# Turning whole float32 words: where a rotated q or k block is split into high and low parts, and how it travels to the stacks

## The chip, the cores and the metric

The kernel runs on one core of one Trainium2 chip. A core has a matrix engine (PE, whose weight loads are shown as a row of their own, PEld), a vector engine (DVE), an activation engine (ACT), a general engine (POOL), a queue engine that only issues transfers (SP), and 16 DMA engines that carry every transfer. The metric is the device time in microseconds of one execution, lower is better. A profile is one execution; the times are medians over several.

## The reference

A transformer block on x of shape 4 x 1024 x 256: attention with 16 heads of width 16 and rotary embedding, then a mixture of 8 experts, with a layer norm and a residual around each. The change touches only the rotated q and k and their way to the score products:

```python
q = (x @ Wq.T + bq).reshape(B, T, H, D)          # H = 16 heads, D = 16
k = (x @ Wk.T + bk).reshape(B, T, H, D)
q = apply_rope(q)                                # x1*cos - x2*sin, x1*sin + x2*cos
k = apply_rope(k)
scores = jnp.einsum('bthd,bshd->bhts', q, k) / np.sqrt(D)
attn = jax.nn.softmax(scores, axis=-1)
out = jnp.einsum('bhts,bshd->bthd', attn, v).reshape(B, T, C)
# then out @ Wo.T + bo, norm, residual, the expert layer, norm, residual
```

## The kernel before

**Tiling.** The attention is cut into 4 batches b, 4 groups g of four heads, and two halves of 512 tokens each. One unit is one (b, g, query half), so there are 32; each unit is done in 8 steps, one per 128 keys, so there are 256 steps (`step`, L709). A step issues on PE the score products `sc` of its four heads (L730), a second small product that subtracts each query's maximum (L736), the products `av` with the values of the step before (L805), and on the average four products `pm` of a unit ahead (L645), whose maxima over keys DVE takes (L648). ACT takes the exponential (L740).

**The stacks.** The score products run in a [...] format (`F32R`), and full precision is had by splitting each float32 word into a high part and a low part and laying both into the contraction: a head's 16 dimensions become 64 rows, q as (high, high, low, low) and k as (high, low, low, high). Those tiles are called stacks. For each (b, g, half) there are two pairs of heads `pr`, and for each pair one stack of q and one of k, of 128 rows x 512 words.

**The way of one half to its stacks**, before the change:

1. `rotated` (L524): five POOL operations on 128 x 512 words (bias, two products with sine, product with cosine, sum) give the tile `rot`, tokens on the partitions. Columns are four heads of q, then four heads of k.
2. `split` (L555): POOL copies `rot` into the even words of the tile `split` in the rounded format (high), then subtracts to get the low words beside them.
3. `stack` (L565): for q and for k separately PE turns four 128 x 128 blocks of interleaved high and low words (L572) into one PSUM bank `ps`, and ACT copies the bank to `half0` or `half1` (L580). A row of it is one dimension of one head, high or low.
4. SP issues ten transfers from SBUF to SBUF that lay those rows into the stacks (L592): per pair of heads, three of 64 rows and two of 32.

The first group (b = 0, g = 0) is done in a start-up stage (`begin`, L1024) with other hands: the rotation on DVE, the high part on ACT and the low part on DVE (`halved`, L1087), and half of the transfers issued from POOL (`fast`). The other 15 groups go through the loop, that is 30 halves.

**What sets the order.** The order on SP, PE, DVE and ACT is written out by hand, by a planner that runs while the kernel is built. A piece of work is a generator: each `yield` names what the next piece costs ("P430 A550" is 430 ns of PE, then 550 ns of ACT; W is a delay), and `run_one` (L452) fits the first due piece that finds its engines free by the planner's own clocks; two PE pieces a step at most (`QUOTA`, L790). `plan_stacks` (L1136) gives each half two pieces, the rotation and the stack: the stack comes after its rotation, the rotation of a half comes after the stack of the same half of the previous group, and both have a due step ahead of the first `pm` that reads the stack. POOL's vector work keeps the program's order (`InOrder`, L132); its transfers are set by the framework's scheduler. SP issues in program order, and on it stand also the copies of weights and empty rows in device memory that the first half of the loop spreads over the steps (L721).

**Buffers.** `rot`, `split`, `half0` and `half1` have two buffers each; PSUM gives four banks to `sc`, `ps` and the other turnings and copies that ACT empties, three to `pm` and what DVE empties, and one to `av`.

Of the kernel before, what the change touches and what calls it, by code (L numbers as in the profile page):

```python
# [8 lines left out]
F32 = mybir.dt.float32  # L9
I32 = mybir.dt.int32  # L10
F32R = mybir.dt.float32r
AF = mybir.ActivationFunctionType
ALU = mybir.AluOpType
# [3 lines left out]
P = 128  # L17
B, T, C = 4, 1024, 256
NH, HD = 16, 16
NG = 4  # L20
# [3 lines left out]
TB = 512  # L24
NTB = TB // P
# [32 lines left out]
def sandwich(  # L58
# [4 lines left out]
    nc = tc.nc  # L63
# [8 lines left out]
    pssc = attn.enter_context(tc.tile_pool(name="pssc", bufs=4, space=PSUM))  # L72
# [5 lines left out]
    ep1 = early.enter_context(tc.tile_pool(name="ep1", bufs=1, side="right"))  # L78
    ep2 = early.enter_context(tc.tile_pool(name="ep2", bufs=2, side="right"))

    def bank(name, pool=ps1):
        return pool.tile([P, TB], F32, tag="bank", name=name)
# [58 lines left out]
    pool = InOrder(nc.gpsimd)  # L141
# [403 lines left out]
        e.tensor_tensor(flat, flat, sw.rearrange("p t h s d -> p (t h s d)"), ALU.add)  # L545
        return c

    splits = {}

    def high_and_low(b, g, half):  # L550
        sp_ = ep2.tile([P, NTB, 8, HD, 2], F32R, tag="split", name=f"split_{b}_{g}_{half}")
        splits[b, g, half] = sp_
        return [sp_[:, :, :, :, l] for l in range(2)]

    def split(b, g, half):  # L555


        yield "G5500"
        c = rotated(b, g, half, pool)
        yield "G2100"  # L560
        hi, lo = high_and_low(b, g, half)
        pool.tensor_copy(hi, c)
        pool.tensor_tensor(lo, c, hi, ALU.subtract)

    def stack(b, g, half, fast=False):  # L565

        halves = []
        for is_k in range(2):
            yield "P430 A550"
            ps = bank(f"ps_{b}_{g}_{is_k}_{half}", pssc).bitcast(F32R)  # L570
            for t in range(NTB):
                nc.tensor.transpose(  # L572
                    ps[:, t * P : (t + 1) * P],
                    splits[b, g, half][:, t, 4 * is_k : 4 * is_k + 4].rearrange(
                        "p h d n -> p (h d n)"
                    ),
                    ident_r,
                )
            m = ep1.tile([P, TB], F32R, tag=f"half{is_k}", name=f"half{is_k}_{b}_{g}_{half}", bufs=2)
            (nc.vector.tensor_copy if fast and is_k else nc.scalar.copy)(m, ps)  # L580
            halves.append(m)
        yield "W8000"
        both = stack_tiles(b, g, half)
        stacks[b, g, half] = both
        for pr in range(2):
            q, k_ = (m[64 * pr : 64 * pr + 64] for m in halves)
            to_q, to_k = both[pr]
            for to, of in (
                (to_k[0::2], k_), (to_q[0::2], q), (to_k[1::4], k_[1::2]), (to_q[1::2], q),
                (to_k[3::4], k_[0::2]),  # L590
            ):
                (nc.gpsimd if fast and pr else nc.sync).dma_start(  # L592
                    out=to.bitcast(F32), in_=of.bitcast(F32)
                )

    def stack_tiles(b, g, half):
        if (b, g) == groups[-1]:
# [426 lines left out]
    def begin():  # L1024

        diag2 = ep1.tile([P, 2, 2, P], F32, tag="B", name="diag2", bufs=2)
        for r in range(2):
            for i in range(2):  # L1030
                nc.vector.tensor_scalar(diag2[:, r, i], ident, bqk_sb[:, i, 0:1], None, ALU.mult)
        pps = [[bank(f"pp_{h}_{n}", pssc) for n in range(2)] for h in range(2)]
        for pp in pps[0] + pps[1]:
            nc.tensor.matmul(
                pp, ones, diag2.rearrange("p r i c -> p (r i c)"), start=True, stop=False
            )
        turned_rope()
        diag = small_constants()
        columns = w2x.rearrange("p (i k) c -> p k i c", k=KC)
        scales = []  # L1040
        for h in range(NQB):
            stats = stats_tile(f"a0_{h}")
            statistics(stats, x_first[h], range(NTB))
            scales.append(norm_scales(stats, NTB, f"a0_{h}", pool if h else nc.vector))

        def normed(h):
            for n in range(2):
                xn = ep2.tile([P, 2, C], F32, tag="rot", name=f"xn_0_{h}_{n}")
                pt = bank(f"pt_0_{h}_{n}").rearrange("p (k t) -> p k t", k=KC)
                for i in range(2):  # L1050
                    normalized(xn[:, i], x_first[h][:, 2 * n + i, :], scales[h], 2 * n + i)
                    for k in range(KC):
                        nc.tensor.transpose(
                            pt[:, k, i * P : (i + 1) * P], xn[:, i, k * P : (k + 1) * P], ident
                        )
                nT = ep2.tile([P, KC, 2 * P], F32, tag="nT", name=f"nT_0_{h}_{n}", bufs=4)
                (nc.scalar.copy if h else nc.vector.tensor_copy)(nT, pt)
                norm[0, h * 2 + n] = nT

        def products(h, n):  # L1060
            for i in range(2):
                for k in range(KC):
                    nc.tensor.matmul(
                        pps[h][n][:, i * 2 * P : (i + 1) * 2 * P],
                        norm[0, h * 2 + n][:, k, i * P : (i + 1) * P], columns[:, k, :, :P],
                        start=False, stop=(i, k) == (1, KC - 1),
                    )


        parts = [  # L1070
            x_first[h].rearrange("p t (h s d) -> p t h s d", h=8, s=2) for h in range(NQB)
        ]
        cs = {}

        def times(h, n):
            t0 = h * NTB + 2 * n
            nc.vector.tensor_tensor(
                parts[h][:, 2 * n : 2 * n + 2].rearrange("p t h s d -> p t h (s d)"),
                pps[h][n].rearrange("p (t h d) -> p t h d", t=2, d=2 * HD),
                turn[:, t0 : t0 + 2, None, :].to_broadcast([P, 2, 8, 2 * HD]), ALU.mult,  # L1080
            )

        def rotation(h):
            cs[h] = ep2.tile([P, NTB, 8, HD], F32, tag="rot", name=f"rot_0_0_{h}")
            nc.vector.tensor_tensor(cs[h], parts[h][:, :, :, 0], parts[h][:, :, :, 1], ALU.add)

        def halved(h):  # L1087
            hi, lo = high_and_low(0, 0, h)
            nc.scalar.copy(hi, cs[h])
            nc.vector.tensor_tensor(lo, cs[h], hi, ALU.subtract)  # L1090

        normed(0)
        for n in range(2):
            products(0, n)
            times(0, n)
        rotation(0)
        normed(1)
        halved(0)
        products(1, 0)
        times(1, 0)  # L1100
        for _ in stack(0, 0, 0, fast=True):
            pass
        compact()
        products(1, 1)
        times(1, 1)
        rotation(1)
        halved(1)
        for h in range(NQB):
            turned[h] = turned_tile(0, h)
            others.append(Work(project(0, h, range(NTB), 1), h - 2))  # L1110
        for _ in range(2):
            others[0].run()
        for _ in stack(0, 0, 1, fast=True):
            pass
        turned_bias(diag)
        others[0].finish()
        matrices_of_maxima()
        for v in v_aug:
            pool.memset(v, 0.0)
            pool.memset(v[:, :, HD : HD + 1], 1.0)  # L1120
        for g in range(NG):
            for j in range(4):
                p0 = g % 2 * 64 + j * HD
                nc.sync.dma_start(
                    out=wo_sb[p0 : p0 + HD, g // 2, :], in_=wo[g, 32 * j : 32 * j + HD, :]
                )
        n = R2 - FR - 1
        nc.sync.dma_start(
            out=wall[:, FR + 1 : R2, OR:].rearrange("e p w -> p e w"),
            in_=zero[:n, None, :C].to_broadcast([n, NE, C]),  # L1130
        )
# [4 lines left out]
    def plan_stacks():  # L1136
        for k, (b, g) in enumerate(groups):
# [4 lines left out]
            for h in range(NQB):  # L1142
                deps = []
                deps.append(stacking[(*groups[k - 1], h)])
                if h:
                    deps.append(splitting[b, g, 0])
                if k == 1:
                    deps.append(others[h])
                if g == 0 and b:
                    preparing[b, h] = Work(  # L1150
                        prepare(b, h), drawing[b, g] - 22 + 6 * h,
                        after=[splitting[(*groups[k - 1], h)]]
                        + ([preparing[b, 0]] if h else []),
                    )
                    deps.append(preparing[b, h])
                splitting[b, g, h] = Work(
                    split(b, g, h), drawing[b, g] - (16 if g == NG - 1 else 6), after=deps
                )
            for h in range(NQB):

# [457 lines left out]
```

## Time and profile before

| quantity | value |
|---|---|
| time, median of 3 runs | 1631.56 us (1630.38 to 1631.83) |
| the profiled execution's own time | 1639.77 us |
| its span, first to last instruction | 1638.0 us |
| instructions | 27716 |
| DVE, ACT, POOL busy, share of the span | 64%, 52%, 31% |
| mean share of the 16 DMA engines, all transfers on SP's queue | 42.1% |

How to read it. A row of groups gives the line, engine and operation, output and inputs by tile name, the shape and the number of instructions, then their busy time together and the mean of one, and last the idle time of the engine just before them with what ended it. Matmuls overlap each other on PE, so the busy time of a group is less than its count times its mean; what one piece of work really costs on a full PE is read from a timeline, as the distance from its start to the start of what follows. The span falls into a start-up until 60 us, the attention loop until about 1030 us, the expert tiles until about 1580 us and a tail.

Busy time by stage, from the view by windows (us of each engine):

| stage | PE | DVE | ACT | POOL | DMA share |
|---|---|---|---|---|---|
| 60 to 1030 | 933.90 | 755.64 | 689.17 | 368.85 | 0.41 |
| 1030 to 1580 | 548.58 | 218.32 | 132.05 | 100.28 | 0.59 |
| 1580 to 1638 | 1.14 | 41.67 | 16.16 | 0.96 | 0.56 |

### The profile page before, as it was taken

How to read it: one execution, taken by the hardware profiler on the slowest of the kernel's cores; microseconds unless marked ns; L12 is line 12 of the kernel's file. 1: busy time of each engine (PE TensorE's matmuls, PEld its weight loads, DVE VectorE, ACT ScalarE, POOL GpSimd, SP SyncE). 2: the span in 40 equal slices, each digit the busy share in tenths (PEclk: the TensorE clock that was granted, in tenths of full speed). 3: DMA queues.
4: the chain of work that ended last, by engine and by line, in shares of the span. 5: the costliest groups of instructions: out<-in, count | busy, mean ns of one | idle time of the engine just before them, and what ended most of it. 6: DMA issues, size and time to landing. Idle time of an engine off the chain costs nothing. (4 is left out here: it accounts for less than half of the span.)

```text
span 1638.0 us, 27716 instructions
## 1 busy us (share of the span) xinstructions
PE 1532.8 (94%) x9456; PEld 1004.4 (61%) x9456; DVE 1046.5 (64%) x2511; ACT 854.8 (52%) x1754; POOL 513.2 (31%) x951
## 2 busy tenths in 40 slices
PE   7889999999999999999999999999999999999960
PEld 4444455645545554445554444788888888899950
DVE  4686788787788787868788883434434433334348
ACT  3366777677777767767677667322311111222213
POOL 6652152254372344462243112133230111111100
PEclk9899999999999999999999999999999999999985
DMA  4299887246054232212141042145455555788855
GB/s 121 90 247 237 236 237 186 85 117 177 12 132 136 75 103 80 53 52 65 37 94 40 1 159 87 66 167 203 179 183 195 195 194 221 251 312 300 304 226 199
DMA packets 114036, 247.94 MB, mean 151 GB/s; under 512 B 16772, under 2 KB 76967, under 8 KB 108007
## 3 DMA queue, kind: packets, MB, share of 16 engines
q1 hardware_dynamic: 103287, 215.47, 42.1%
q0 software_dynamic: 9120, 26.38, 4.9%
q10 hardware_dynamic: 1488, 4.33, 0.7%
q8 instruction: 75, 1.23, 0.3%
q14 instruction: 66, 0.54, 0.1%
HBM read 149.18 MB, written 80.73 MB: 140 GB/s over the span
## 5 line engine op out<-in xcount | busy, mean ns | idle before, releaser
L648 DVE TENSOR_REDUCE part<-pm 128x1 f32<-128x512 f32 x1024 | 640.5, 683 | 134.1 <-PE pm L645 132.1
L740 ACT ACTIVATE e<-sc 128x512 f32<-128x512 f32 x1024 | 530.2, 604 | 149.0 <-PE sc L736 147.5
L1330 PE MATMUL pu<-xT,w 128*128 128x256 f32 (+3 forms) x2024 | 359.9, 333 | 2.4 <-DMA w<-wall 1.2
L1330 PEld LDWEIGHTS pu<-xT,w 128*128 128x128 f32 (+1 forms) x2024 | 313.7, 190 | 33.2 <-issue 1.6
L1336 ACT ACTIVATE sil<-pu,w 128x256 f32<-128x256 f32 (+3 forms) x276 | 117.1, 425 | 415.9 <-PE pu L1330 392.9
L645 PE MATMUL pm<-stack,stack 64*128 64x512 f32 x992 | 282.5, 465 | 15.0 <-DVE part L648 11.9
L805 PE MATMUL av<-e,v 128*32 128x512 f32 x2048 | 274.9, 606 | 0.3 <-ACT e L740 0.3
L1341 DVE SCALAR_TENSOR_TENSOR h<-pu,w,sil 128x256 f32<-128x256 f32 (+1 forms) x230 | 97.2, 423 | 221.5 <-ACT sil L1336 220.6
L645 PEld LDWEIGHTS pm<-stack,stack 64*128 64x128 f32 x992 | 136.5, 185 | 162.1 <-DVE part L648 111.1
L730 PE MATMUL sc<-stack,stack 64*128 64x512 f32 x992 | 220.1, 405 | 4.1 <-ACT half L580 3.6
L736 PE MATMUL sc<-shift,bring 64*128 64x512 f32 x1024 | 222.7, 398 | 0.5 <-ACT shift L632 0.2
L1377 POOL DMA_INDIRECT res<-yo,ids x71 | 68.8, 969 | 411.7 <-DVE yo L1376 406.3
L1364 PE MATMUL pe<-w,h 128*128 128x256 f32 x710 | 167.5, 383 | 0.0
L1364 PEld LDWEIGHTS pe<-w,h 128*128 128x128 f32 x710 | 132.6, 190 | 25.4 <-issue 8.3
L730 PEld LDWEIGHTS sc<-stack,stack 64*128 64x128 f32 x992 | 113.8, 186 | 37.9 <-ACT e L740 15.0
L736 PEld LDWEIGHTS sc<-shift,bring 64*128 64x128 f32 x1024 | 105.7, 185 | 21.4 <-ACT shift L632 5.2
L1376 DVE TENSOR_SCALAR yo<-pe,xt 128x256 f32<-128x256 f32 x71 | 34.4, 484 | 90.3 <-PE pe L1364 90.2
L805 PEld LDWEIGHTS av<-e,v 128*32 128x32 f32 x2048 | 40.8, 108 | 71.1 <-issue 65.5
L992 POOL DMA_INDIRECT rows<-xr,to x64 | 62.6, 978 | 55.9 <-DVE to L987 34.6
L139 POOL TENSOR_TENSOR t_y<-y_y 128x4 f32<-128x4 f32 x24 | 4.7, 197 | 182.2 <-DVE y_y L334 181.0
L503 PE MATMUL pp<-wqk,nT 128*128 128x512 f32 (+1 forms) x128 | 61.1, 604 | 0.0
L139 POOL TENSOR_TENSOR rot<-turned,bias_qk 128x512 f32<-128x512 f32 x30 | 39.2, 1307 | 67.0 <-ACT turned L508 66.9
(297 smaller groups left out, 1396.2 us busy)
## 6 DMA issues: line engine op xcount, KB each, us to landing
w<-wall SPq DMA_DIRECT2D x46, 2034.0 KB
rows<-empty SPq DMA_DIRECT2D x35, 1032.0 KB
stack<-half SPq DMA_DIRECT2D x186, 128.0 KB
stack<-half SPq DMA_DIRECT2D x124, 64.0 KB
xt<-rows SPq DMA_DIRECT2D x25, 258.0 KB
wall<-in_wg_dram SPq DMA_DIRECT2D x16, 342.0 KB
wall<-in_w_dram SPq DMA_DIRECT2D x16, 320.0 KB
wall<-in_w_dram SPq DMA_DIRECT2D x8, 640.0 KB
```

The lines of the kernel that those rows point to most:

```text
L645: nc.tensor.matmul(pm, q[r, i * P : (i + 1) * P], k_[r], start=True, stop=True)
L648: nc.vector.tensor_reduce(part[:, i, 2 * pr + s, half : half + 1], pm, AX.X, ALU.max)
L730: nc.tensor.matmul(sc, k_[r, kt : kt + P], q[r], start=True, stop=False)
L736: nc.tensor.matmul(scs[s], bring[pr][r, :], shift[u][r, :], start=False, stop=True)
L740: nc.scalar.activation(e, scs[s], AF.Exp, scale=1.0 / HD**0.5)
L805: nc.tensor.matmul(av[32 * j : 32 * j + 32, :], v_aug[kb][:, 4 * g + j, :], es[j], start=(kb == 0), stop=(kb == NT - 1),)
L992: sent = nc.gpsimd.indirect_dma_start(out=rows[:, :], out_offset=bass.IndirectOffsetOnAxis(ap=to[:, i, t : t + 1], axis=0), in_=xr[:, t, i ...
L1330: nc.tensor.matmul(pu[:m, i, :n], w[:, c0 : c0 + m], xT[:, k, :n], start=(k == 0), stop=(k == KC - 1),)
L1336: nc.scalar.activation(sil[:m, :n], pu[:m, 0, :n], AF.Silu, bias=w[:m, OB + f : OB + f + 1])
L1341: nc.vector.scalar_tensor_tensor(h[:, f, :n], pu[:, 1, :n], bias, sil[:, :n], ALU.add, ALU.mult)
L1364: nc.tensor.matmul(po[:, :C], hs[j % 2][:, f, i * P : (i + 1) * P], w[:, O2 + f * C : O2 + (f + 1) * C], start=False, stop=(f == NC - 1),)
L1377: sent = nc.gpsimd.indirect_dma_start(out=res[:, :], out_offset=bass.IndirectOffsetOnAxis(ap=ids, axis=0), in_=y, in_offset=None,)
```

## The change

The split moves behind the turning. The rotated tile is turned as float32 words, all eight blocks of heads at once: four turnings of 128 x 128 into one PSUM bank instead of eight into two. In the loop ACT copies the bank to a new tile `full`, and POOL then makes the high part `part0` and the low part `part1` from it. In the start-up ACT rounds the bank straight into `part0`, and DVE subtracts it from the bank into `part1`; `halved` goes away. A row of `part0` or `part1` is one dimension of one head, so a pair of heads has 32 rows of q and 32 of k in each, and every quarter of every stack is one transfer: 16 transfers of 32 rows for each half, k before q, where there were six of 64 rows and four of 32. The bytes that they carry are the same. The stack's second piece now asks the planner for POOL time.

```diff
-    def high_and_low(b, g, half):
-        sp_ = ep2.tile([P, NTB, 8, HD, 2], F32R, tag="split", name=f"split_{b}_{g}_{half}")
...
-    def split(b, g, half):
+    def rotate(b, g, half):
         yield "G5500"
-        c = rotated(b, g, half, pool)
-        yield "G2100"
-        hi, lo = high_and_low(b, g, half)
-        pool.tensor_copy(hi, c)
-        pool.tensor_tensor(lo, c, hi, ALU.subtract)
+        rots[b, g, half] = rotated(b, g, half, pool)

     def stack(b, g, half, fast=False):
-        halves = []
-        for is_k in range(2):
-            yield "P430 A550"
-            ps = bank(f"ps_{b}_{g}_{is_k}_{half}", pssc).bitcast(F32R)
-            for t in range(NTB):
-                nc.tensor.transpose(
-                    ps[:, t * P : (t + 1) * P],
-                    splits[b, g, half][:, t, 4 * is_k : 4 * is_k + 4].rearrange(
-                        "p h d n -> p (h d n)"
-                    ),
-                    ident_r,
-                )
-            m = ep1.tile([P, TB], F32R, tag=f"half{is_k}", name=f"half{is_k}_{b}_{g}_{half}", bufs=2)
-            (nc.vector.tensor_copy if fast and is_k else nc.scalar.copy)(m, ps)
-            halves.append(m)
-        yield "W8000"
+        yield "P540 A550"
+        ps = bank(f"ps_{b}_{g}_{half}", pssc)
+        for t in range(NTB):
+            nc.tensor.transpose(
+                ps[:, t * P : (t + 1) * P],
+                rots[b, g, half][:, t].rearrange("p h d -> p (h d)"), ident,
+            )
+        parts = [
+            ep2.tile([P, TB], F32R, tag=f"part{i}", name=f"part{i}_{b}_{g}_{half}") for i in range(2)
+        ]
+        if fast:
+            nc.scalar.copy(parts[0], ps)
+            nc.vector.tensor_tensor(parts[1], ps, parts[0], ALU.subtract)
+        else:
+            full = ep2.tile([P, TB], F32, tag="full", name=f"full_{b}_{g}_{half}")
+            nc.scalar.copy(full, ps)
+            yield "G2100 W9600"
+            pool.tensor_copy(parts[0], full)
+            pool.tensor_tensor(parts[1], full, parts[0], ALU.subtract)
         both = stack_tiles(b, g, half)
         stacks[b, g, half] = both
         for pr in range(2):
-            q, k_ = (m[64 * pr : 64 * pr + 64] for m in halves)
-            to_q, to_k = both[pr]
-            for to, of in (
-                (to_k[0::2], k_), (to_q[0::2], q), (to_k[1::4], k_[1::2]), (to_q[1::2], q),
-                (to_k[3::4], k_[0::2]),
-            ):
-                (nc.gpsimd if fast and pr else nc.sync).dma_start(
-                    out=to.bitcast(F32), in_=of.bitcast(F32)
-                )
+            for is_k in (1, 0):
+                r = slice(64 * is_k + 32 * pr, 64 * is_k + 32 * pr + 32)
+                for n, low in enumerate(((0, 0, 1, 1), (0, 1, 1, 0))[is_k]):
+                    (nc.gpsimd if fast and pr else nc.sync).dma_start(
+                        out=both[pr][is_k][n::4].bitcast(F32), in_=parts[low][r].bitcast(F32)
+                    )
...
         def rotation(h):
-            cs[h] = ep2.tile([P, NTB, 8, HD], F32, tag="rot", name=f"rot_0_0_{h}")
-            nc.vector.tensor_tensor(cs[h], parts[h][:, :, :, 0], parts[h][:, :, :, 1], ALU.add)
-
-        def halved(h):
-            hi, lo = high_and_low(0, 0, h)
-            nc.scalar.copy(hi, cs[h])
-            nc.vector.tensor_tensor(lo, cs[h], hi, ALU.subtract)
+            rots[0, 0, h] = ep2.tile([P, NTB, 8, HD], F32, tag="rot", name=f"rot_0_0_{h}")
+            nc.vector.tensor_tensor(rots[0, 0, h], parts[h][:, :, :, 0], parts[h][:, :, :, 1], ALU.add)
...
-        halved(0)
...
-        halved(1)
...
                 splitting[b, g, h] = Work(
-                    split(b, g, h), drawing[b, g] - (16 if g == NG - 1 else 6), after=deps
+                    rotate(b, g, h), drawing[b, g] - (16 if g == NG - 1 else 6), after=deps
                 )
```

More of the change, by code (lines that the diff above doesn't have):

```diff
@@ L546, in rotated @@
         return c
-    splits = {}
-    def high_and_low(b, g, half):
-        sp_ = ep2.tile([P, NTB, 8, HD, 2], F32R, tag="split", name=f"split_{b}_{g}_{half}")
-        splits[b, g, half] = sp_
-        return [sp_[:, :, :, :, l] for l in range(2)]
-    def split(b, g, half):
-        yield "G5500"
-        c = rotated(b, g, half, pool)
-        yield "G2100"
-        hi, lo = high_and_low(b, g, half)
-        pool.tensor_copy(hi, c)
-        pool.tensor_tensor(lo, c, hi, ALU.subtract)
-    def stack(b, g, half, fast=False):
-        halves = []
-        for is_k in range(2):
-            yield "P430 A550"
-            ps = bank(f"ps_{b}_{g}_{is_k}_{half}", pssc).bitcast(F32R)
-            for t in range(NTB):
-                nc.tensor.transpose(
-                    ps[:, t * P : (t + 1) * P],
-                    splits[b, g, half][:, t, 4 * is_k : 4 * is_k + 4].rearrange(
-                        "p h d n -> p (h d n)"
-                    ),
-                    ident_r,
-                )
-            m = ep1.tile([P, TB], F32R, tag=f"half{is_k}", name=f"half{is_k}_{b}_{g}_{half}", bufs=2)
-            (nc.vector.tensor_copy if fast and is_k else nc.scalar.copy)(m, ps)
-            halves.append(m)
-        yield "W8000"
+    rots = {}
+    def rotate(b, g, half):
+        yield "G5500"
+        rots[b, g, half] = rotated(b, g, half, pool)
+    def stack(b, g, half, fast=False):
+        yield "P540 A550"
[17 more added lines that the diff above has]
+            pool.tensor_tensor(parts[1], full, parts[0], ALU.subtract)
         both = stack_tiles(b, g, half)
@@ L1072, in begin @@
         ]
-        cs = {}
         def times(h, n):
```

## The prediction

> **What bounds the kernel.** I read the stages by windows first, the groups of PE next, then the timeline of a few steps of the loop. In the loop PE is busy 933.90 of 970 us, in the expert stage 548.58 of 550; DVE comes second with 755.64 of 970. Whether a full PE is really the limit is seen in a step:
>
> ```profile
> 502.64 0.53 PE L572 MATMUL ps<-ident_r,split 128*128 128x128 f32 x4
> 503.10 0.50 PE L645 MATMUL pm<-stack,stack 64*128 64x512 f32 x2
> 503.44 0.39 PE L730 MATMUL sc<-stack,stack 64*128 64x512 f32 x2
> ...
> 504.81 1.06 PE L805 MATMUL av<-e,v 128*32 128x512 f32 x8
> 505.81 0.53 PE L572 MATMUL ps<-ident_r,split 128*128 128x128 f32 x4
> 506.27 0.50 PE L645 MATMUL pm<-stack,stack 64*128 64x512 f32 x2
> ```
>
> No row carries a wait, each piece begins as the one before drains, and the step from 502.64 to 505.81 lasts 3.17 us. Without the turning L572 it would be 3.17 - 0.46 = 2.71, which is what the step from 508.97 to 511.68 shows. So a PE piece taken out of the loop shortens it, until DVE (four maxima of about 0.62 us, 2.48 a step) comes near. How seldom PE waits stands in the groups:
>
> ```profile
> L645 PE MATMUL pm<-stack,stack 64*128 64x512 f32 x992 | 282.5, 465 | 15.0 <-DVE part L648 11.9
> L730 PE MATMUL sc<-stack,stack 64*128 64x512 f32 x992 | 220.1, 405 | 4.1 <-ACT half L580 3.6
> L572 PE MATMUL ps<-ident_r,split 128*128 128x128 f32 x240 | 34.3, 267 | 4.2 <-POOL split L139 4.1
> ```
>
> The column behind the last bar is PE's idle time: 12 us for DVE in the whole run, 3.6 for a PSUM bank that ACT's copy of a turned half holds, 4.1 for POOL's split.
>
> **The change part by part.**
>
> *Turning (L572).* 240 turnings in the loop are 60 banks of four; a bank costs 0.46 us from its start to the `pm` behind it, so a half costs 0.92-0.93. The change has one bank per half, of unrounded float32. The trace has that form: L675 turns four 128 x 128 float32 blocks.
>
> ```profile
> 475.57 0.66 PE L675 MATMUL pd<-ident,ou 128*128 128x128 f32 x4
> 476.16 0.51 PE L645 MATMUL pm<-stack,stack 64*128 64x512 f32 x2
> ```
>
> That is 0.59; others of L675, L827 and L483 before a `pm` give 0.53 to 0.57 where nothing else waits. I take 0.56: 0.93 - 0.56 = 0.37 saved a half, times 30 = **-11.1 us**; ends 0.34 and 0.47, so -10 to -14.
>
> Here a rule speaks against the change. The Trainium skill (FP8 and Floating Point Precision, "TensorE Precision Notes") says that true float32 takes four passes through the array, where the reduced format takes one. By the rule a float32 bank would cost 4 x 0.46 = 1.84 us (an estimate from that page), a half would lose 0.9 us, and 30 halves +27 us. The row decides: 0.53 to 0.59, a factor near 1.2, not 4, for a turning.
>
> *ACT.* One copy of a bank (about 0.59 us) less per half. ACT has room (689 of 970), so the time itself is worth nothing; but the bank waits of 3.6 us (five in the loop: 1.56 at 97.61, the others 0.43 to 0.71) come from two `ps` banks per half among four. One bank instead of two: I take half, **-1.8** (ends 0 and -3.6).
>
> *POOL's split moves behind the turning.* Its cost stays (cast 0.65, subtraction 1.30, a little under 2 us). In front of PE it goes away:
>
> ```profile
> 459.13 0.54 PE L572 MATMUL ps<-ident_r,split 128*128 128x128 f32 x4 [1.72 <-POOL split L139]
> ...
> 723.54 0.53 PE L572 MATMUL ps<-ident_r,split 128*128 128x128 f32 x4 [2.35 <-POOL split L139]
> ```
>
> With the rotation alone to wait for, POOL is done 2 us earlier; but the planner puts the turning earlier as well. I take half of 4.1, **-2** (ends +2 and -4). The new wait is on POOL: its cast waits for ACT's copy, and behind it stand the next rotations, the small operations of the norms and the indirect writes of rows. Such a block is there already, because the split's two buffers are held by PE:
>
> ```profile
> POOL split L139 <- PE ps L572: 68.6, 4, 26.4
> POOL rot L139 <- ACT turned L508: 66.9, 7, 25.9
> ...
> SPq L592 <- ACT half L580: 274.7, 22, 48.3
> ```
>
> These are total, times, longest. The same turning ends POOL's wait before and after, so it is replaced and not added. With POOL at 369 of 970 us its queue catches up.
>
> *Transfers.* Ten issues become sixteen on SP, and what waits behind them is the bulk copying of L721. The shortest cover is that of the first group:
>
> ```profile
> 79.88 6.23 SPq L592 DMA_DIRECT2D stack<-half  x10
> 86.16 0.59 SPq L721 DMA_DIRECT2D rows<-empty  x1
> 87.39 8.39 SPq L592 DMA_DIRECT2D stack<-half  x10
> ```
>
> Ten issues take 6.2 us, 8.4 where bulk copies fill the DMA engines (0.91 of their time from 90 to 120). Sixteen at the same pace are 10.0 and 13.4. The first set ends near 89, the second near 104. Their first `pm` stand at 101.93 and 113.46; landing took 2.0 to 4.2 us where the trace shows it (POOL's issues), and a bulk copy of 1 MB in front adds some 4. Cover left: 5 us and 2 us at worst. From the second group on, 37 to 84 us lie between the last issue and the first `pm`. So the six added issues cost **0**; without that cover the second set would stall PE for what it is late, a few us, once.
>
> The skill's other rule here (DMA: Bandwidth & Descriptors, "Rules for kernel authors") is to coalesce small transfers, since each carries a fixed 2 us. Priced serially, 6 x 30 x 2 = 360 us (an estimate from that page); by the rows an added issue is 0.6 us of SP, which idles 275 us in L592 alone. The rows decide.
>
> *Start-up.* ACT and DVE each lose one operation of about 0.69 per half, PE turns 0.6 instead of 0.84 and need not wait for the split (0.32 and 0.49), so PE reaches its first `pm` about 1 us before 35.39. POOL then issues eight transfers per half instead of five, at 0.53 each with a 1.86 us memset between: the last of half 0 leaves near 33.3, lands near 36.6, and the third `pm` waits 1 to 2 us. Together **0** (ends -1.5 and +2).
>
> *What is late next.* DVE. Its share in the loop is 78%, so I give back a fifth of what PE saves on it, **+2.4**.
>
> Sum: -11.1 - 1.8 - 2 + 0 + 2.4 = **-12.5 us** against 1639.77, that is 1627.3, or 0.76%. The expert stage is full on PE and shifts as it is. The median before is 1631.56, so the forecast is **1619 us**.
>
> **The rivals.**
>
> *No change to speak of: DVE takes the saving.* In favour: in units with norms and routing DVE has its own work beside 2.48 us of maxima per step, and a `pm` waits for its bank. Against: only 12 us of PE idle time end in DVE. If DVE took four fifths of the saved time, 2.5 us would be left: 1629. Chance 0.10.
>
> *Slower: PE meets late rotations.* One mechanism, at the turning of L572. POOL runs in program order, and each rotation of a group now comes behind the split of the group before, which waits for PE and ACT; before, the five operations of the rotation ran ahead and only the split waited. A rotation then starts when the last turning is done, and PE, in order too, stands at the next until it is there. The price is that of the two rows above, about 2 us a time. It decides from about 7 of 30 halves on (14 us); at half of them it is 15 x 2 - 12.5 = some +17, 1649. Against: in about three of four halves 20 to 60 us lie between the end of the split and its turning (rows of POOL's tile `split` against rows of L572), so a later start has room. Chance 0.12.
>
> *Stacks late in the first group only.* By the second set above, if its last transfers land 5 us behind their `pm` at 113 us: 1619 + 5 = 1624. Chance 0.13; still faster.
>
> *It doesn't do what it says* hardly arises: the count of turnings is in the code.
>
> **How the numbers follow.** Forecast 0.65 (own range 1612 to 1625), late first stacks 0.13, no change 0.10, late rotations 0.12. The measurement tells 0.2%, 3.3 us, from nothing. Faster: 0.65 + 0.13 = 0.78; within: 0.10; slower: 0.12. The range holds the forecast, the late first stacks and the no-change case: 1610 to 1632. Its low end is the sum of the good ends: -14 - 3.6 - 4 - 1.5 + 2.4 = -20.7.
>
> **What would show it.** Right: 120 turnings of L572's successor in the loop at about 0.56 us per bank, a loop shorter by 10 to 15 us in the stage up to 1030, no PE wait before `pm` at the first group, POOL's busy time unchanged, SP's issues still near 0.6 us. Wrong: PE idle before the turning ended by POOL's `rot` in many halves, idle before `pm` or `sc` that grows by ten us or more (DVE), or a bank of float32 turnings near 0.9 us or above.

## The result, and the profile after

The change makes the kernel slower: 1684.22 us (median of 6 runs, 1680.22 to 1686.84) against 1631.69 (6 runs, 1630.38 to 1637.47), a ratio of 1.0315 [1.0302, 1.0328]. The profiled execution took 1686.84 us with a span of 1685.0; its PE clock averaged 0.959 of full speed, where before it was 0.976. The expert stage only shifts: from the last `av` to the last `pe` lie 552.9 us after and 555.3 before. The loss lies in the attention loop, whose span from the first to the last `av` went from 951.2 to 1004.9 us, +53.7. (The first `av` also came 4.0 us sooner, at 70.50 for 74.54; but in b_lin below, whose start-up is that of before, it stands at 70.95, so this is not put down to the change.) "In the loop" means between these two `av` from here on, with the gaps under 0.15 us that the view of waits leaves out.

The groups of the profile after that answer to those shown before:

```profile
L636 PE MATMUL pm<-stack,stack 64*128 64x512 f32 x992 | 284.0, 475 | 35.1 <-DVE part L639 30.2
L721 PE MATMUL sc<-stack,stack 64*128 64x512 f32 x992 | 218.4, 415 | 0.0
L561 PE MATMUL ps<-ident,rot 128*128 128x128 f32 x128 | 22.0, 300 | 18.6 <-POOL rot L139 18.6
L139 POOL CAST part<-full 128x512 fp32r<-128x512 f32 x30 | 18.4, 613 | 129.4 <-ACT full L573 86.6 <-DMA rows<-empty 34.5 <-DMA stack<-part 8.3
```

Half as many turnings; the wait of `sc` for ACT's copies is gone; but the idle time before `pm` went from 15.0 to 35.1 and that before the turning from 4.2 to 18.6. PE's own waits, first of the kernel before, then of the one after (total us, times, longest):

```profile
PE pm L645 <- DVE part L648: 12.8, 30, 1.1
PE pmx L628 <- DVE mx L624: 10.0, 8, 1.8
...
PE ps L572 <- POOL split L139: 4.1, 2, 2.4
PE sc L730 <- ACT half L580: 3.6, 5, 1.6
```

```profile
PE pm L636 <- DVE part L639: 30.6, 32, 4.6
PE ps L561 <- POOL rot L139: 18.6, 4, 8.1
PE pbias__3509 L258 <- DMA lined<-lin: 18.1, 1, 18.1
PE pmx L619 <- DVE mx L615: 10.1, 6, 1.8
```

Three rows carry the loss: a few waits for DVE's maxima (`part`) of up to 4.6 us where none was over 1.1; four for a rotation; and one of 18.1 us for a transfer that the prediction never named.

**The four late rotations.** The timeline of POOL and PE at the first of them:

```profile
71.50 0.66 PE L561 MATMUL ps<-ident,rot 128*128 128x128 f32 x4
...
72.84 0.61 POOL L139 CAST part<-full 128x512 fp32r<-128x512 f32 x1 [16.00 <-ACT full L573]
73.53 1.28 POOL L139 TENSOR_TENSOR part<-full,part 128x512 fp32r<-128x512 f32 x1
74.76 1.30 POOL L139 TENSOR_TENSOR rot<-turned,bias_qk 128x512 f32<-128x512 f32 x1
...
78.95 1.26 POOL L139 TENSOR_TENSOR rot<-rot,sw 128x512 f32<-128x512 f32 x1
...
80.26 1.12 PE L561 MATMUL ps<-ident,rot 128*128 128x128 f32 x4 [4.82 <-POOL rot L139]
```

POOL stood 16 us in front of the cast until PE had turned that half and ACT had copied it; only then came the five operations of the next rotation, and PE, in order, stood at its turning. The next turning, at 87.60, waits 2.68 us more while POOL, busy without a pause, works off the same backlog. These two are the mechanism of the slower rival. The other two late rotations, 2.95 and 8.11 us, are not:

```profile
204.07 1.31 POOL L139 TENSOR_TENSOR rot<-turned,bias_qk 128x512 f32<-128x512 f32 x1 [25.87 <-ACT turned L508]
...
209.60 1.05 PE L561 MATMUL ps<-ident,rot 128*128 128x128 f32 x4 [2.95 <-POOL rot L139]
```

```profile
852.50 0.85 POOL L139 DMA_DIRECT2D xb<-in_x_dram  x1
853.35 0.62 POOL L139 CAST part<-full 128x512 fp32r<-128x512 f32 x1
...
860.75 1.12 PE L561 MATMUL ps<-ident,rot 128*128 128x128 f32 x4 [8.11 <-POOL rot L139]
```

At 204.07 POOL had waited for the rotation's own input; the rotation takes 5.5 us from there, and PE is free for its turning at 206.65. At 853.35 no split waits; the rotation, begun at 855.28, stands behind residual sums, splits and a norm's small operations that POOL does one after another since 840.00.

**The transfer.** SP's queue before, then after (start, duration from the first to the last issue of a row, number of issues):

```profile
255.38 6.24 SPq L592 DMA_DIRECT2D stack<-half  x10
...
263.02 8.59 SPq L592 DMA_DIRECT2D stack<-half  x10
271.71 1.06 SPq L249 DMA_DIRECT2D lin<-flat  x2
275.72 0.30 SPq L253 DMA_DIRECT2D lined<-lin  x1
```

```profile
232.53 35.77 SPq L712 DMA_DIRECT2D rows<-empty  x12
268.42 27.45 SPq L583 DMA_DIRECT2D stack<-part  x32
...
297.29 2.35 SPq L249 DMA_DIRECT2D lin<-flat  x2
303.67 0.30 SPq L253 DMA_DIRECT2D lined<-lin  x1
```

`lined` is the experts' biases on their way to a turning of PE (L258). Before, its transfer was issued at 275.72 and PE turned it at 281.29 without a wait. After, two sets of stacks are 32 issues instead of 20, the queue is late by 28 us, and PE stands for 18.1.

**The clock.** The clock record of the trace shows half speed for 3.4 us of the loop before and 71.7 after, in stretches of 3.4 us or a multiple. They stand behind the waits (windows: start:end, length, PE, PEld, DVE, ACT and POOL busy, granted clock, DMA share, GB/s):

```profile
291.60:312.10 20.50, 6.49 (x30) 3.85 (x30) 2.15 (x4) 2.74 (x7) 0.00 (x0) 0.50 0.52 127
349.70:356.50 6.80, 4.94 (x21) 2.30 (x21) 5.92 (x15) 0.61 (x2) 6.56 (x8) 0.50 0.94 286
854.80:865.00 10.20, 4.25 (x20) 2.75 (x24) 1.53 (x3) 2.11 (x5) 7.49 (x8) 0.50 0.46 134
```

The first is the wait for `lined`, the second one for DVE, the third the longest one for a rotation.

So the 53.7 us come apart: PE idle in the loop 31.2 before and 80.4 after, +49.2; PE busy 920.0 and 924.5, +4.5. If the turnings took some 11 us off the busy time, as the prediction's sum has it, about 16 came back; against x2_again below, which runs the same instructions on PE and is busy 913.0 us, it is 11.5. The clock is enough for either: PE was busy in 48.5 of the 71.7 us at half speed (before, in all 3.4), and there two products of a step stand 0.43 us apart (355.17 and 355.60) where at full speed it is 0.24 (472.42 and 472.66). 45.1 x (1 - 0.24 / 0.43) is an estimate of 20 us if every piece stretched so.

### The profile page after: what moved, and what is told of

Read it like the earlier page. It is cut to its first block, busy times and chain, and to the rows that moved or that the text cites. A ratio compares the mean times of both kernels' runs of the same rounds, so it can differ in the third digit from the quotient of the medians.

```text
span 1685.0 us, 27669 instructions
## 1 busy us (share of the span) xinstructions
PE 1530.3 (91%) x9328; PEld 1001.5 (59%) x9328; DVE 1054.4 (63%) x2509; ACT 838.2 (50%) x1722; POOL 515.0 (31%) x957
## 5 line engine op out<-in xcount | busy, mean ns | idle before, releaser
L636 PE MATMUL pm<-stack,stack 64*128 64x512 f32 x992 | 284.0, 475 | 35.1 <-DVE part L639 30.2
L721 PE MATMUL sc<-stack,stack 64*128 64x512 f32 x992 | 218.4, 415 | 0.0
L721 PEld LDWEIGHTS sc<-stack,stack 64*128 64x128 f32 x992 | 112.3, 193 | 26.9 <-ACT e L731 11.8
L139 POOL CAST part<-full 128x512 fp32r<-128x512 f32 x30 | 18.4, 613 | 129.4 <-ACT full L573 86.6
```

Of the source, the lines that this page charges most:

```text
L636: nc.tensor.matmul(pm, q[r, i * P : (i + 1) * P], k_[r], start=True, stop=True)
L721: nc.tensor.matmul(sc, k_[r, kt : kt + P], q[r], start=True, stop=False)
```

## The experiments

Ratios are against the kernel before on the same chip. **A plan** here means the order and place that the planner gives to all pieces of the loop. In a_lin, b_16 and b_lin that order is, on PE, DVE and ACT, the one of the kernel that they are made from; in x1_plan it is that of before less the operations that went. The traces bear this out: without the turnings and their copies, DVE and ACT run the same operations in the same order, and PE differs by swaps of neighbouring products alone.

**The transfer alone, and another hand for the split** (both from the kernel after).

```diff
# a_lin
-            nc.sync.dma_start(            # lin, twice
+            nc.gpsimd.dma_start(
-        lined = cl.tile([2 * NE, FF], F32, tag="xr", name="lined")
-        nc.sync.dma_start(out=lined, ...)
+        lined = cl.tile([2 * NE, FF], F32, tag="lined", name="lined")
+        nc.gpsimd.dma_start(out=lined, ...)
```

> The changed kernel with the three transfers that turn the biases (lin, lin, lined; L249 and L253) issued from POOL instead of SP, and with a buffer of its own for lined, so that they no longer stand behind SP's bulk copies and stack transfers, nor wait for the last copy of empty rows. PE, DVE and ACT keep their order. Theory (SP's queue is late): the one wait of 18.1 us at 305 us goes, and with it most of the 20 us of half clock around it, worth some 8 us more: about 1658 us. Rival (the order of the planner costs the time, and the wait only stands where something else would wait): above 1675 us.

Measured 1669.6 us, 1.0219 [1.0198, 1.0240]. The wait for `lined` is gone, worth about 15 us (1.0315 less 1.0219), and the rest stays: PE waits 30.4 us for `part`, 14.6 for rotations, half clock is 71.7 us. The time lies between the theory and the rival: more than two thirds of the loss have another cause.

```diff
# a_dve
-            full = ep2.tile([P, TB], F32, tag="full", ...)
-            nc.scalar.copy(full, ps)
-            yield "G2100 W9600"
-            pool.tensor_copy(parts[0], full)
-            pool.tensor_tensor(parts[1], full, parts[0], ALU.subtract)
+            nc.scalar.copy(parts[0], ps)
+            yield "D700 W9600"
+            nc.vector.tensor_tensor(parts[1], ps, parts[0], ALU.subtract)
```

> The changed kernel with the split in the loop made straight from PSUM, the high part by ACT and the low part by DVE, as in the start-up; POOL has no part in a stack. The 16 transfers on SP stay. Theory (POOL's queue holds the next rotations behind a cast that waits for the turning): PE's waits for rot fall from 18.6 us to under 5, and its waits before pm from 31 to about 15, since POOL's other work comes in time; the wait for lined stays: about 1655 us, in spite of 21 us more of DVE work. Rival (the transfers or the planner's order alone are at fault): 1680 us or more.

Measured 1706.25 us, 1.0451 [1.0422, 1.0480]: a miss. POOL is out of the way, and rotations are still late three times (9.5 us), while `sc` now waits 25.9 us for ACT's `e`. The pieces had changed once more and with them the plan, so the run can't tell POOL's part from the plan's.

**The kernel before with one thing added.** Sixteen transfers of 32 rows in place of ten; the order on PE, DVE and ACT is that of before:

```diff
# b_16
-        yield "W8000"
+        yield "W9600"
-                (to_k[0::2], k_), (to_q[0::2], q), (to_k[1::4], k_[1::2]), (to_q[1::2], q),
-                (to_k[3::4], k_[0::2]),
+                (to_k[0::4], k_[0::2]), (to_k[1::4], k_[1::2]), (to_k[2::4], k_[1::2]),
+                (to_k[3::4], k_[0::2]), (to_q[0::4], q[0::2]), (to_q[1::4], q[0::2]),
+                (to_q[2::4], q[1::2]), (to_q[3::4], q[1::2]),
```

> The kernel before with each transfer of 64 rows cut into two of 32, so 16 per half on SP, k before q, and W9600 for W8000; split and turning as they were. Theory (SP's queue): the last copy of empty rows is issued near 290 us instead of 262, and PE waits 10 to 20 us for lined; nothing else: 1645 to 1660 us. Rival (the added issues are hidden, the loss comes from POOL and the planner): 1632 us within 5.

Measured 1654.54 us, 1.0134 [1.0109, 1.0158]: six more issues a half cost 21 us, within the theory's range. Its "nothing else" is wrong, as PE's waits show:

```profile
PE sc L731 <- ACT half L580: 10.3, 6, 4.4
PE pbias__3591 L258 <- DMA lined<-lin: 8.4, 1, 8.4
```

The second is the transfer again; SP issued `lin` at 291.24 where before it was 271.71. The first is a second way for a late queue to reach PE: ACT's copy waits for a `half` buffer that undelivered transfers still hold (9.1 us, the longest 5.0), and PE for its bank at 89.20 (3.84 us) and at 103.55 (4.42). Half clock rises from 3.4 to 27.3 us.

Then two numbers of the planner alone, those that the change also has, with every instruction kept:

```diff
# b_plan
-            yield "P430 A550"
+            yield "P540 A550"
-        yield "W8000"
+        yield "W9600"
```

> The kernel before with the planner's costs alone changed: P540 for P430 at both turnings and W9600 for W8000. The instructions are the same, their order on the engines is not. Theory (queues): within 8 us of 1632. Rival (any new plan costs tens of us, and the old one was a lucky one): above 1645 us.

Measured 1657.47 us, 1.0150 [1.0125, 1.0175]: +24 us with not one instruction added, and the theory that the plan hardly matters falls. PE waits for `part` 22.3 us in the loop, the longest 3.3 (before 12.9 and 1.1), and half clock is 34.1 us:

```profile
PE pm L645 <- DVE part L648: 21.8, 32, 3.3
PE ps L572 <- POOL split L139: 4.9, 2, 2.5
```

The waits for DVE are the pattern of the kernel after. The waits at the turning are about those of before (4.1 us), so these 24 us do not come from turnings put too early.

**The change on the plan of before.** The kernel after with the old pieces: the numbers of before, and empty pieces where the second turning and the split were.

```diff
# x1_plan, from the kernel after
         rots[b, g, half] = rotated(b, g, half, pool)
+        yield "G2100"
...
-        yield "P540 A550"
+        yield "P430 A550"
...
-            yield "G2100 W9600"
+            yield "P430 A550"
+            yield "W8000"
```

> The changed kernel with the planner's pieces of the kernel before (rotation G5500 and an empty G2100; stack P430 A550 with the four turnings and the copy, an empty P430 A550, then W8000 with POOL's split and the 16 transfers), so that PE, DVE and ACT keep the order of the kernel before, less the operations that the change removes. Theory A (three parts: a new plan, some 24 us as b_plan showed; SP's queue, some 21 as b_16 showed; the split's place on POOL for the rest; less 11 for the turnings): with the plan taken out, 1645 to 1660 us. Theory B (the split's place on POOL is the main part): 1665 us or more. Theory C (the plan is all of it): 1635 us or less.

x2_lin adds the edit of a_lin to it:

> x1_plan with the biases' three transfers on POOL's queue and lined in a buffer of its own, as in a_lin. Theory A: 8 to 15 us below x1_plan, that is 1632 to 1648, with waits for late rotations left over. Theory B: within 5 us of x1_plan.

x3_free adds to x2_lin four `rot` buffers and takes the split out of POOL's fixed order (`nc.gpsimd` for `pool` in the two lines of the split):

> x2_lin with four buffers for rot and with the split on POOL taken out of the fixed program order, so that the framework's scheduler may put a rotation ahead of a split that still waits; the order on PE, DVE, ACT and SP is the same. If the order on POOL makes rotations late: PE's waits at the turning for rot fall to 5 us or less and the time falls by what they were in x2_lin, together with the half clock that follows them, to about 1625 us. If PE's waits have other causes: within 4 us of x2_lin.

Measured: x1_plan 1657.9, 1.0025 [1.0004, 1.0046]; x2_lin 1636.86, 0.9896 [0.9857, 0.9934]; x3_free 1645.55, 0.9951 [0.9930, 0.9971]. On this chip the kernel before took 1653.96 us (1648.11 to 1660.77), so only ratios are carried from it. x1_plan's time lies in theory A's range only because of that; its ratio, 4 us above the kernel before, is nearer to theory C, that the plan is nearly all. x2_lin gains more than theory A gave it, and x3_free does neither of the things that were expected. With the old plan, late rotations fall to 0.3 us, so they came with the plan; the transfer still costs 21 us (x1 to x2, one wait of 13.5 us and what follows it); and freeing the split loses: PE waits 6.4 us for `xr` of ACT, which it did not in x2_lin.

Since that chip took longer for the kernel before, the main kernels ran again on another, with the kernel before under a label of its own, and the kernel before with the edit of a_lin as b_lin:

> The kernel before once more, with a profile on the chip of this set. On the chip of the last set it took 1654 us where two other chips gave 1632. If that chip's transfers are slower and lined is late there too, and this set runs on such a chip, a wait before the turning of lined shows here; on a chip as the first, 1632 us and no such wait.

> The changed kernel once more, on the chip of this set, so that every other run of the set has its own measure: 1.03 of ctl on a chip as the first; if ctl itself waits for lined, the ratio is nearer 1.02.

> x2_lin (the change, the plan of the kernel before, the biases' transfers on POOL's queue) once more. Theory A: its gain in the last set was the biases' way, that is, about 1635 us on any chip, so 1.00 of ctl on a chip as the first and 0.99 on a slow one. If the turnings' 11 us are kept: 0.993 or less on both.

> The kernel before with the biases' three transfers on POOL's queue and lined in a buffer of its own, nothing else. Theory A: where ctl shows no wait for lined, within 4 us of ctl; where it shows one, faster by that wait. x2_again less b_lin is then what the change itself is worth once plan and lined are out: 0 to -8 us.

Measured against 1633.07 us: ctl 1.0001 [0.9990, 1.0013], after_again 1.0315 [1.0298, 1.0332], x2_again **0.9910 [0.9893, 0.9926]** (1619.45 us), b_lin 1.0002 [0.9991, 1.0013]. Clearing the transfer alone is worth nothing in the kernel before, where nothing waited for it; so x2's gain is the change's own. Four runs make a square of plan and transfer: the old plan takes off 0.029 with the transfer in the way (after to x1_plan) and 0.031 without (a_lin to x2_again); clearing the transfer takes off 0.010 on the new plan and 0.013 on the old. That is 47 to 50 us for the plan and 16 to 21 for the transfer, with ratios from several chips. The waits of x2_again and a step with a turning:

```profile
PE pm L638 <- DVE part L641: 14.4, 31, 1.7
PE pmx L621 <- DVE mx L617: 7.1, 7, 1.8
PE pp L1027 <- DVE diag L1024: 6.5, 1, 6.5
PE pt L1046 <- ACT xn L365: 2.1, 2, 1.2
```

```profile
481.50 0.66 PE L562 MATMUL ps<-ident,rot 128*128 128x128 f32 x4
482.08 0.50 PE L638 MATMUL pm<-stack,stack 64*128 64x512 f32 x2
```

No wait for a rotation, a copy or a transfer is among the large ones; a half costs one bank of 0.58 us; half clock in the loop is 6.8 us; the loop takes 936.7 us, 14.5 less than before, of which PE's idle time is 7.5 (31.2 to 23.7) and its busy time 7.0 (920.0 to 913.0).

**Which of the pieces does it.** From x2, one number or piece at a time set as the change has it: the first cost P540 for P430 (y1_p540), no empty second PE piece (y2_one), no empty POOL piece after the rotation (y3_rot), the last piece `"G2100 W9600"` for `"W8000"` (y4_g). No instruction differs in kind or number.

> x2_lin (1619 us) with one number of the plan changed: the first piece of a stack asks for P540 instead of P430. Theory D (every plan but the one of the kernel before opens waits of 2 us and more, each with half clock behind it; the place of the turning does not matter): 1630 us or more. Theory E (the harm is that the turning is put in front of its rotation): within 6 us of 1619, since the pieces stay.

> x2_lin without the empty second piece P430 A550 of a stack, so that a stack is one PE piece as in the change. Theory E: the next half's turning moves up behind the last one, PE waits for rot 10 us or more in all, 1640 us or more, most of the way to a_lin (1669). Theory D: 1630 us or more without such waits.

> x2_lin without the empty piece G2100 behind the rotation, as in the change. Theory E: the turning may come 2 us sooner, some waits for rot, below 5 us; 1619 to 1628 us. Theory D: 1630 us or more.

> x2_lin with G2100 W9600 for W8000 at the last piece of a stack, as in the change, so that the planner books POOL's split where it is. Theory E: POOL's bookings are now true, so no more waits than x2_lin, within 6 us of 1619. Theory D: 1630 us or more.

Measured against 1633.55 us, with the distance to x2's 0.991 in us:

| | us | ratio | from x2 | PE waits for `part` / rotations in the loop | half clock |
|---|---|---|---|---|---|
| y1_p540 | 1637.86 | 1.0023 [1.0009, 1.0038] | +18 | 23.2 / 5.0 | 17.1 |
| y2_one | 1656.91 | 1.0150 [1.0133, 1.0167] | +39 | 23.3 / 9.6 | 41.0 |
| y3_rot | 1626.51 | 0.9970 [0.9956, 0.9985] | +10 | 18.4 / 2.2 | 13.7 |
| y4_g | 1620.49 | 0.9924 [0.9906, 0.9942] | +2 | 13.4 / 3.6 | 17.1 |

Neither theory holds throughout. E (the harm is the turning put in front of its rotation) has y3 and y4 and the time of y2, but y1 costs 18 us where it gave 6. D (every other plan costs) has y1 and y2 and fails at y4: there PE's order differs from x2's in dozens of places, and it costs 2 us. The largest cost is that of the missing second piece, and its largest wait is a late rotation, one turning of the new shape:

```profile
829.42 1.11 PE L562 MATMUL ps<-ident,rot 128*128 128x128 f32 x4 [7.73 <-POOL rot L139]
```

These four costs sum to 69 us, where all four together cost about 50 (a_lin's 1.0219 against 0.991), so they don't add up.

## Why the prediction was wrong

It said 1619 us and faster with 0.78; the time was 1684. Its sum was made for a kernel in which only the counted instructions change. x2 is that kernel, with the transfer's way cleared, and took 1619.45 us where the kernel before took 1633.07. That the sum, 12.5, comes so close to 13.6 is in part luck: smaller and larger terms offset each other. The prediction's own sign of being wrong, idle time before `pm` that grows by ten us or more, came true (15.0 to 35.1). By its steps:

- **Turning, -11.1: right.** One bank of 0.58 us at 481.50, so 0.93 - 0.58 = 0.35 a half and 10.5 in all (the busy time of x2's loop fell by 7.0, with 3.4 us more of half clock); the skill's rule of four passes was rightly set aside for the row.
- **ACT's bank waits, -1.8: right in sign.** The row `sc` behind a copy (3.6 us) is gone in the kernel after and in x2: -3.6, the good end.
- **POOL's split, -2: failed in the kernel after.** The wait before the turning went from 4.2 to 18.6 us. On the old plan it went to 0.3, -3.9, the good end.
- **"The planner puts the turning earlier as well": the step that failed most.** It gives the planner 2 us within one term (its end of +2) and treats the order of everything else as given. The change takes a PE piece per half away, gives another cost to the one that stays, and moves POOL's time, so all of the loop is planned anew. That costs about 50 us (a_lin against x2: same instructions and the same cleared transfer). And b_plan, which changes two of the numbers and nothing else, loses 24. A new order need not cost anything, as y4 shows; but it must be priced.
- **"So it is replaced and not added": wrong where it counts.** Before, POOL waited with its split, and the rotation was done; after, POOL waits with the split and the rotation is still to come. The rival priced it at about 2 us and asked for 7 halves of 30; rotations were late 4 times, by 2.7 to 8.1 us, and only the first two stood behind a split that waited for PE.
- **DVE, +2.4: far too small for the kernel after,** where PE's waits for `part` rise by 18 us (12.9 to 30.8). In x2 they rise by 2.4 (to 15.3), but those for `mx` fall by 2.9 (8.6 to 5.7 in the loop), so DVE took next to nothing there. The rows at 351.56 show where one wait comes from:

```profile
348.86 1.27 POOL L139 TENSOR_TENSOR xb<-xb,outs 128x512 f32<-128x512 f32 x1
...
350.17 0.75 DVE L371 BATCH_NORM_STATS2 st_m<-xb 128x6 f32<-128x256 f32 x2 [5.11 <-POOL xb L139]
...
350.84 2.46 DVE L639 TENSOR_REDUCE part<-pm 128x1 f32<-128x512 f32 x4
...
351.56 0.79 PE L636 MATMUL pm<-stack,stack 64*128 64x512 f32 x1 [4.58 <-DVE part L639]
```

  DVE waits 5.11 us for a residual sum on POOL, the maxima stand behind it, and PE, whose `pm` has no bank, stands 4.58. The long waits at 600.51 and 842.70 have such waits of DVE for `xb` before them too; those at 431.06, 504.63 and 679.95 have none, there DVE was busy with work of its own that the order had put in front. So it was the order, on POOL and on DVE, and not DVE's share of busy time, that set the price.

- **Transfers, 0: wrong, 15 to 21 us.** The cover of the stacks was read rightly: no `pm` of the loop waited for a stack, and 23 us or more lay between the last issue of a set and the first `pm` that reads it. The sentence "what waits behind them is the bulk copying of L721" left out L249 and L253, three issues of another stage on the same queue, which PE waits for. The estimate of 360 us by the rule on coalescing was far too high.
- **Start-up, 0: as worked out, as far as these rows show.** The first `pm` came at 33.87 instead of 35.39, and the third waited 1.18 us for its stack.
- **The clock was not in the sum.** Each wait was priced by its length; some 12 to 16 us of the loss, by the account of busy time, are put down to work done at half clock behind the waits.

Left open: how the plan's cost divides between the turning's place (y2 speaks for it) and the order of the rest (b_plan loses 24 us without a late turning); why one chip ran the kernel before in 1654 us; and by which order on POOL x3 lost. A plan made afresh for the new pieces, better than x2's borrowed one, was not tried.

## What to carry to other kernels

Where an order is planned from costs written by hand, an edit of a piece's cost or count is an edit of the whole order: hold the order fixed, with empty pieces if need be, to see what the edit itself is worth, and plan again only then. When issues are added to a queue that is already full, list every instruction behind them to the end of the full stretch, those of other stages too, with who waits for each and what holds its buffer. And price a wait on a nearly full PE with the slow clock that may follow it.

## What the runs showed of the hardware

- Waits far shorter than the half-clock stretch can bring it on. In the kernel after, waits of 1.86 us (ended 504.63), 1.81 (441.66) and 1.58 (679.95) were followed by half clock at 506.7, 441.8 and 680.8, 3.4 us each; the longer one at 600.51 was not:

```profile
441.66 0.64 PE L619 MATMUL pmx<-ident_r,mx 128*128 128x128 f32 x4 [1.81 <-DVE mx L615]
600.51 0.49 PE L636 MATMUL pm<-stack,stack 64*128 64x512 f32 x1 [3.14 <-DVE part L639]
```

  In each of the 17 traces, all changes of the granted clock lie on one grid of 3.41 us, and what counts is PE's idle time within one period of it. The wait at 441.66 lies in one period; that at 600.51 is cut into 1.47 and 1.67. Of the periods at full speed from 75 to 1600 us of all traces, those with over 1.7 us of idle time were followed by half clock in 74 of 75 cases, those with 1.1 to 1.7 in 32 of 116, those with less in 2 of 4022. So the same wait can cost half clock in one execution and not in the next: the kernel before waits 1.72 us at 459.13 without it, b_lin, which is the same on PE, 1.73 us at 455.04 with it (455.5). The Trainium skill (TensorE: Matmul & The Clock Gate, "HAM oscillation — how this bites in real kernels") sets the bound at idle gaps above about 3.4 us; here that is too lax.
- Turning a bank of float32 costs little more than one of the rounded format: 0.58 us (481.50 to 482.08) against 0.46 (502.64 to 503.10 in the kernel before).
- An issue on SP takes about 0.6 us (6.24 / 10 in the row at 255.38), and 35.77 / 12 = 3.0 us for a 1 MB copy where the DMA engines are full (their share is 1.05 in the view by windows from 232 to 268 us of the kernel after).
